# Placing the projection's x tiles first, loading the attention output from ScalarE's queue, and reordering the last four weighing steps

## The chip, the cores and the metric

The kernel runs on one core of a Trainium2 chip. The metric is the device time of one execution in microseconds, as the median of several runs. A core has five engines that run on their own instruction streams: TensorE (PE, matmuls), VectorE (DVE), ScalarE (ACT), GpSimd (POOL) and SyncE (SP). Transfers are issued by SP, ACT or POOL, each on a queue of its own and in the order of its stream, and are carried out by 16 DMA engines that all queues share. An engine that has to wait before it may issue a transfer holds up everything behind it in its stream.

## What is computed

The input `x` has 48 channels of 256 x 256 pixels. Layer 0 normalizes it over groups of channels, makes q, k and v by a pointwise and a depthwise convolution, cuts them into patches of 4 x 4 pixels (4096 tokens), runs 8 heads of attention over the tokens, folds the patches back and projects the result. Layer 1 normalizes again and multiplies along columns, rows and channels in windows of 64. Both layers add their input:

```python
x = x + _L0_conv_ref(_gn(x), w_qkv, w_dw, temperature, w_proj)
    # qkv = dwconv3x3(einsum(x, w_qkv)); q, k l2-normalized per head
    # attn = softmax(einsum('bhcn,bhcm->bhnm', q, k) * temperature)
    # out  = einsum('bhcn,bhnm->bhcm', v, attn); fold; einsum(out, w_proj)
x = x + _L1_conv_ref(_gn(x), Ws, Hs, Cs, 64)
    # einsum('bcphqw,twW,thH,tcC->bCpHqW', windows of x, Ws, Hs, Cs)
```

## The kernel before

The attention takes most of the time. For each of the 8 heads it loops over 16 groups `g` of 256 query tokens; in a group, `scores` (L536) makes the logits (L341) and their exponentials (L545), `normalised` (L554) scales the values (`vn`, L564), and `weigh(h, g, blocks, k)` (L567) multiplies them for `k` = 0 to 3, each `k` covering 1024 of the 4096 tokens (32 matmuls per step, which the trace counts as 64, L574; VectorE adds the result into `oaccs[h, k]`, L585). After the last group of a head, `store(h, m)` (L587) takes 512 tokens at a time, `m` = 0 to 7, where `m` = 2k and 2k + 1 come from step `k`: four transposes (L591), one copy by ScalarE into `oo` (L593; two buffers), and two stores of 96 KB by GpSimd into the DRAM tensor `os_` (L595). In the last group the loop calls `store` one step late (L693): the two pieces of step `k` are stored after step `k + 1`, and pieces 6 and 7 after the loop (L696).

The attention is under a manual schedule: its instructions stand in the order in which they are written. The projection behind it is not: there a scheduler orders each engine's instructions, and derives the waits.

The projection (L702 to L737) runs over 8 tiles `t`. A tile takes 16 rows of each half of the image. Both halves lie side by side on the partitions, 48 channels each, so that a tile has two loads of `pot` (attention output, tile `t` and tile `8 + t` of `os_`; L715) and two of `pxt` (x itself; L716), 768 KB each, all issued by SP. Piece `m` of the attention's store gives tiles 2m and 2m + 1 of `os_`: the first half of tile 0 comes from piece 0, its second half from piece 4. TensorE multiplies (L721), VectorE adds into `pxt` (L728) and takes statistics (L732), and GpSimd stores the two halves of the result into `x1s` (L737), 768 KB each. `pot` and `pxt` have three buffers each in the pool `pj`. Its 96 KB per partition lie, from the bottom up, where the convolution's pool `cv` was (50 KB) and where the attention's pool `ahead` (queries, keys, values) was. The tile that is allocated first lies lowest: `pot` over `cv`, `pxt` over `ahead`.

SP's order as built is: both `pxt` loads of tile 0, the two `pot` loads of tile 0, then tiles 1 and 2 with `pot` and `pxt` in turn; from tile 3 on a `pot` load waits for the matmuls of three tiles before, a `pxt` load for the landing of the x store of three tiles before. Layer 1 (L766 on) begins by reading `x1s` back (L790) once all stores have landed and the statistics are done.

Of the kernel before, what the change touches and what calls it, by code (L numbers as in the profile page):

```python
# [8 lines left out]
F32 = mybir.dt.float32  # L9
# [10 lines left out]
P2 = 2 * C  # L20
# [4 lines left out]
NT = (H // KS) * (W // KS)  # L25
# [13 lines left out]
TP = 256  # L39
# [5 lines left out]
def conv_preact_kernel(  # L45
# [15 lines left out]
    nc = tc.nc  # L61
# [33 lines left out]
    for s in range(2):  # L95
        r = slice(s * C, (s + 1) * C)
        for h in range(NH if s == 0 else H0):
# [3 lines left out]
                in_=w_qkvT.rearrange("c (z h e) -> h c z e", z=3, h=NH)[h],  # L101
# [68 lines left out]
    class Strip:  # L170
# [24 lines left out]
        def store(self):  # L195
            for s, rows in enumerate(both_halves(t1[1], 2 * self.j, 2, base=1)):
                nc.sync.dma_start(out=rows, in_=self.ot[:, 2 * s : 2 * s + 2, :])
# [305 lines left out]
    with tc.tile_pool(name="ahead", bufs=2) as ah, tc.tile_pool(name="ae", bufs=3) as ae, tc.tile_pool(  # L503
# [110 lines left out]
        with tc.manual_schedule():  # L614
            load_query(0, 1)
            block = scores(0, 0)
            for h in range(NH):
                more = h + 1 < NH
                rows = {r: Depthwise(h + 1, r) for r in range(CR + 1)} if more else {}
                for g in range(NG):  # L620
                    p, d, n = rows.get(g - 2), rows.get(g - 1), rows.get(g)

                    if h == 0 and 0 < g <= 6:
                        load_value(0, g + 1)
                    if more and CR + 2 <= g < CR + 6:
                        for m in range(2):
                            load_value(h + 1, (g - CR - 2) * 2 + m)
                    if more and CR + 3 <= g < CR + 6:
                        for m in range(2):
                            load_key(h + 1, (g - CR - 3) * 2 + m)  # L630

                    blocks = [normalised(*block)]
                    block = scores(h, g * G + 1)
                    if more and g == NG - 1:
                        load_key(h + 1, 6)
                        load_key(h + 1, 7, nc.gpsimd)
                    if g + 2 < NG:
                        load_query(h, g + 2)
                    elif more:
                        load_query(h + 1, g + 2 - NG)  # L640
                    if p:
                        p.store((2,))
                    if d:
                        for t in range(1, 4):
                            d.tap(t)
                    second = block
                    if g + 1 < NG:
                        block = scores(h, (g + 1) * G)
                    elif more:
                        block = scores(h + 1, 0)  # L650
                    blocks.append(normalised(*second))
                    if d:
                        for t in range(4, 9):
                            d.tap(t)

                    if g == 0 and rows:
                        rows[0].load()
                    if p:
                        p.high()
                    if d:  # L660
                        d.square()
                    if n:
                        n.first()
                    for k in range(NK):
                        s = (h * NG + g) * NK + k
                        weigh(h, g, blocks, k)
                        if k == 0 and d:
                            d.reduce()
                        if k == 0 and p:
                            p.low(nc.gpsimd)  # L670
                            p.store((0, 1))
                        for w in strips[s]:
                            w.run(big.tile([128, 2, 512], F32, name="big"))
                        for w in strips[s + 2]:
                            w.load()
                        for w in strips[s - 1] if s else []:
                            w.store()
                        if k == 2 and d:
                            d.norm()
                            d.root()  # L680
                        if k == 2 and g + 1 in rows:
                            rows[g + 1].load()
                        if k == 3 and d:
                            d.scale()
                        if h == 0 and 0 < g <= 6 and k == 0:
                            turn(0, g + 1)
                        if more and CR + 2 <= g < CR + 6 and k in (0, 2):
                            turn(h + 1, (g - CR - 2) * 2 + k // 2)

                        if g == 0 and h > 0 and k == 0:  # L690
                            for m in range(6, 8):
                                store(h - 1, m)
                        if g == NG - 1 and k > 0:  # L693
                            for m in range(2 * k - 2, 2 * k):
                                store(h, m)
            for m in range(6, 8):  # L696
                store(NH - 1, m)
    attention.close()
# [5 lines left out]
    with tc.tile_pool(name="pj", bufs=3) as pj, tc.tile_pool(name="pjs", bufs=1) as pjs, tc.tile_pool(  # L704
        name="pps", bufs=3, space=PSUM
    ) as pps, tc.tile_pool(name="pp1", bufs=1, space=PSUM) as pp1:
        st1 = pjs.tile([P2, HALF * W // 512, 6], F32, name="st1")
        ov = os_.rearrange("t (c k) n -> t c k n", k=KK)
        for t in range(HALF // RP):
            ot = pj.tile([P2, KK, NP], F32, name="pot")  # L710
            xt = pj.tile([P2, RP, W], F32, name="pxt")
            for s in range(2):
                r = slice(s * C, (s + 1) * C)
                y0 = s * HALF + t * RP
                nc.sync.dma_start(out=ot[r], in_=ov[s * (NT // 2 // TP) + t])  # L715
                nc.sync.dma_start(out=xt[r], in_=xc[:, y0 : y0 + RP, :])  # L716
            xv = xt.rearrange("p (py ki) (px kj) -> p ki kj py px", ki=KS, kj=KS)
            for ki in range(KS):
                ps = pps.tile([P2, KS, NP], F32, name="pps")
                for i in range(0, KS, 2):  # L720
                    nc.tensor.matmul(  # L721
                        ps[:, i : i + 2, :],
                        lhsT=wp,
                        rhs=ot[:, ki * KS + i : ki * KS + i + 2, :],
                        start=True,
                        stop=True,
                    )
                nc.vector.tensor_add(  # L728
                    xv[:, ki], ps.rearrange("p k (py px) -> p k py px", py=RP // KS), xv[:, ki]
                )  # L730
            for i in range(0, RP, 2):
                nc.vector.bn_stats(  # L732
                    st1[:, (t * RP + i) // 2, :], xt[:, i : i + 2, :].rearrange("p a b -> p (a b)")
                )
            for s in range(2):
                y0 = s * HALF + t * RP
                nc.gpsimd.dma_start(out=x1s[:, y0 : y0 + RP, :], in_=xt[s * C : (s + 1) * C])  # L737

        gm2 = pjs.tile([P2, 64 + C], F32, name="gm2")
        nc.vector.memset(gm2, 0.0)  # L740
        for o in (0, 64):
            nc.vector.tensor_copy(gm2[:, o : o + C], gm[:, 0:C])
        mv1, e1 = group_stats(st1, mean1, rstd1, pjs, pp1)
        pc1 = pp1.tile([64 + C, 1], F32, name="pc1", tag="pstat")
        nc.tensor.matmul(pc1, lhsT=gm2, rhs=e1, start=True, stop=True)
        rstd2 = l1c.tile([64 + C, 1], F32, name="rstd2")
        nc.vector.tensor_scalar_add(rstd2, pc1, EPS)
        nc.scalar.activation(rstd2, rstd2, AF.Sqrt)
        nc.vector.reciprocal(rstd2, rstd2)

        csn = l1c.tile([64 + C, T3 * C], F32, name="csn")
        for s in range(2):
            nc.scalar.dma_start(
                out=csn[s * 64 : s * 64 + C].rearrange("c (t d) -> c t d", t=T3), in_=Cs.rearrange("t c d -> c t d")
            )
            r = slice(s * 64, s * 64 + C)
            nc.vector.tensor_scalar_mul(csn[r], csn[r], rstd2[r])
        mrow = pjs.tile([C, 128], F32, name="mrow")
        nc.vector.tensor_scalar_mul(mrow, ones, mean1[0:C])
        pb1 = pp1.tile([128, T3 * C], F32, name="pb1")  # L760
        nc.tensor.matmul(pb1, lhsT=mrow, rhs=csn[0:C], start=True, stop=True)
        cbias = l1c.tile([128, T3 * C], F32, name="cbias")
        nc.vector.tensor_copy(cbias, pb1)
# [176 lines left out]
```

## Time and profile before

| | us |
|---|---|
| median of 3 runs (3782.36, 3788.41, 3791.38) | 3788.41 |
| profiled execution | 3789.12 |
| its span, first to last instruction | 3787.3 |
| last logits matmul (L341) ends | 3289.27 |
| first matmul of the projection (L721) | 3321.47 |
| last statistics of the projection end (L138 begins) | 3467.71 |
| first load of layer 1 issued (L790) | 3472.86 |

PE is busy 3511.2 us of the span (93%), DVE 2201.6, ACT 1719.0, POOL 599.8. In the projection TensorE's share falls to about half, and its matmuls wait 8 times, 68.3 us in total, for `pot`. A row of the timeline gives the start in us, the duration, the engine (SPq, ACTq: the time in which a queue issued transfers), the line, the operation with output and input tile, how many instructions were merged, and in brackets the idle time before it with what ended it.

### The profile page before, as it was taken

Reading aid. Unit: us, or ns where it says so; the run is one execution under the profiler, and the core shown is the slowest. Engines: PE = TensorE matmul, PEld = TensorE weight load, DVE = VectorE, ACT = ScalarE, POOL = GpSimd, SP = SyncE. Lnnn points to the kernel's source line nnn. Section 1 sums busy time; section 2 is a strip of 40 time slices with the busy share of each in tenths; the row PEclk is TensorE's granted clock in tenths of the full one; section 3 lists DMA queues with packets and bytes.
Section 4 is the critical chain, followed back from the end, with each engine's and each line's share of the span. In section 5 each row is a group of like instructions: output and inputs, shape, how many; then the busy total and the mean of one; then the engine's idle time right before and its main releaser. Section 6 shows DMA issues by size and latency. Waiting matters only on the chain.

```text
span 3787.3 us, 99981 instructions
## 1 busy us (share of the span) xinstructions
PE 3511.2 (93%) x44216; PEld 2913.1 (77%) x44216; DVE 2201.6 (58%) x3520; ACT 1719.0 (45%) x2668; POOL 599.8 (16%) x595
## 2 busy tenths in 40 slices
PE   1867999999999999999999999999999999955998
PEld 0225777788888888888888888888888889812776
DVE  5572775169727962895299439934992222266564
ACT  0224665555545554555455445545554444300222
POOL 0030121012301220121122112211220000000011
PEclk9888999999999999999999999999999999966999
DMA  6575666534533542354244424432443100299784
GB/s 138 168 177 153 185 192 172 167 110 118 116 83 99 125 110 75 104 127 106 81 109 117 100 83 117 116 98 76 123 114 93 41 21 19 44 243 188 122 145 90
DMA packets 307459, 441.64 MB, mean 117 GB/s; under 512 B 98298, under 2 KB 232778, under 8 KB 302792
## 3 DMA queue, kind: packets, MB, share of 16 engines
q1 hardware_dynamic: 253590, 270.32, 27.5%
q0 software_dynamic: 48320, 156.61, 18.5%
q10 hardware_dynamic: 5106, 8.21, 1.0%
q8 instruction: 351, 5.75, 0.6%
q14 instruction: 92, 0.75, 0.1%
HBM read 234.76 MB, written 199.95 MB: 115 GB/s over the span
## 4 chain that ended last, share of the span: by engine, by line
PE 82%; DMA 6%; issue 2%; DVE 1%; SPq 1%; ACT 0%; POOL 0%; ACTq 0%; POOLq 0%
PE big L341 36%; PE big L574 35%; PE pb L838 4%; PE pa L816 2%; PE pc L855 2%; PE big L185 1%; DMA pad<-t 1%; DMA x1s<-pxt 1%; PE pt L591 1%; PE pst L528 1%; DMA pxt<-in_x_dram 1%; DMA pot<-os__70 1%; DMA t<-ot 1%; PE pn L255 1%; DMA qkv<-ol 0%
## 5 line engine op out<-in xcount | busy, mean ns | idle before, releaser
L545 ACT ACTIVATE e<-big,nmx 128x1024 f32<-128x1024 f32 x1024 | 1144.3, 1118 | 842.1 <-PE big L341 631.7
L341 PE MATMUL big<-kt,qt 128*128 128x512 f32 x6144 | 1438.5, 393 | 43.9 <-DMA qt<-qkv 29.9
L574 PEld LDWEIGHTS big<-vn,e 128*64 128x64 f32 x32768 | 1367.6, 137 | 86.1 <-ACT e L545 45.1
L574 PE MATMUL big<-vn,e 128*64 128x96 f32 x32768 | 1425.4, 248 | 7.5 <-ACT ot L188 4.1
L341 PEld LDWEIGHTS big<-kt,qt 128*128 128x128 f32 x6144 | 1145.4, 188 | 306.5 <-issue 44.6
L585 DVE TENSOR_TENSOR oacc<-big,oacc 128x768 f32<-128x768 f32 x480 | 458.2, 955 | 706.2 <-PE big L574 706.2
L236 DVE SCALAR_TENSOR_TENSOR acc<-pad,dwt,acc 126x1024 f32<-126x1024 f32 x600 | 777.2, 1296 | 33.6 <-ACT acc L217 17.2
L294 POOL TENSOR_TENSOR ol<-o,oh 126x1024 fp32r<-126x1024 f32 x80 | 189.4, 2368 | 942.2 <-DVE ss L251 804.7
L558 DVE TENSOR_REDUCE zt<-zs 128x1 f32<-128x4 f32 x256 | 39.0, 152 | 361.3 <-ACT e L545 361.3
L545 ACT ACTIVATION_READ_ACCUMULATOR e<-big,nmx 128x1 f32 x1024 | 196.0, 191 | 0.0
L823 DVE TENSOR_TENSOR lzt<-pa,cbias 128x864 f32<-128x864 f32 (+1 forms) x88 | 137.0, 1627 | 99.7 <-PE pa L816 99.7
L845 ACT COPY lyt<-pb 128x512 f32<-128x512 f32 x144 | 84.5, 586 | 215.7 <-PE pb L838 215.7
L299 POOL DMA_DIRECT2D qkv<-o x70 | 86.1, 1231 | 511.0 <-DVE zu L560 243.6
L595 POOL DMA_DIRECT2D os__70<-oo x128 | 65.1, 515 | 594.0 <-ACT oo L593 593.6
L247 ACT ACTIVATE sq<-acc 126x1024 f32<-126x1024 f32 x75 | 79.3, 1058 | 167.8 <-issue 112.2
L281 DVE TENSOR_TENSOR o<-acc,y 126x1024 f32<-126x1024 f32 x75 | 149.4, 1992 | 0.1
L838 PEld LDWEIGHTS pb<-wsb,lzt 128*64 128x64 f32 x2304 | 126.3, 138 | 29.2 <-issue 21.2
L838 PE MATMUL pb<-wsb,lzt 128*64 128x128 f32 x2304 | 142.7, 280 | 2.5 <-issue 2.4
L721 PE MATMUL pps<-pot,wp 96*96 96x512 f32 x128 | 77.9, 776 | 68.3 <-DMA pot<-os__70 68.3
L188 ACT ACTIVATE ot<-big,bias 108x1024 f32<-108x1024 f32 x64 | 71.1, 1112 | 153.9 <-PE big L185 72.0
L217 ACT ACTIVATE acc<-pad,dwt 126x1024 f32<-126x1024 f32 x75 | 85.3, 1137 | 73.3 <-DMA pad<-t 73.3
L721 PEld LDWEIGHTS pps<-pot,wp 96*96 96x96 f32 x128 | 26.6, 215 | 119.1 <-issue 118.6
(115 smaller groups left out, 1888.4 us busy)
## 6 DMA issues: line engine op xcount, KB each, us to landing
pad<-t SPq DMA_DIRECT2D x80, 761.9 KB
qkv<-ol POOLq DMA_DIRECT2D x80, 504.0 KB, 8.9
qkv<-o POOLq DMA_DIRECT2D x70, 504.0 KB, 6.9
qkv<-oh POOLq DMA_DIRECT2D x70, 504.0 KB, 7.4
t<-ot SPq DMA_DIRECT2D x128, 217.7 KB
qt<-qkv SPq DMA_DIRECT2D x176, 96.0 KB
xs<-in_x_dram SPq DMA_DIRECT2D x128, 96.0 KB
os__70<-oo POOLq DMA_DIRECT2D x128, 96.0 KB, 2.2
```

Of the source, the lines that this page charges most:

```text
L217: nc.scalar.mul(self.acc, self.pad[:, 0:KS, 0:W], dwt[:, self.h, 0:1])
L236: nc.vector.scalar_tensor_tensor(self.acc, self.pad[:, dy : dy + KS, dx : dx + W], dwt[:, self.h, tap : tap + 1], self.acc, ALU.mult, ALU.add,
L281: nc.vector.tensor_tensor(self.o.rearrange("p (a b) x -> p a b x", a=KS), self.acc.rearrange("p a (x b) -> p a b x", b=KS), self.y.rearran ...
L294: eng.tensor_sub(self.ol, self.o, self.oh.bitcast(F32))
L299: eng.dma_start(out=qkv[self.h][i].rearrange("j (c k) n -> (j c) k n", k=KK)[:, :, px], in_=self.o if i == 2 else (self.ol if i else self. ...
L341: nc.tensor.matmul(ps[:, i, :], lhsT=qt[:, r, q0 : q0 + 128], rhs=kts[2 * j + i][:, r // 2, :], start=(r == 0), stop=(r == 2),)
L545: nc.scalar.activation(e[:, j * 1024 : (j + 1) * 1024], ps.rearrange("p a b -> p (a b)"), AF.Exp, bias=nmx[:, b : b + 1], accum_out=zs[:, ...
L574: nc.tensor.matmul(ps[p : p + 64, j // 4, j % 4 * HD : (j % 4 + 1) * HD], lhsT=e[:, mb * 128 + p : mb * 128 + p + 64], rhs=vn, start=(i == 0),
L585: nc.vector.tensor_add(oaccs[h, k], ps[:, :, : 4 * HD], oaccs[h, k])
L721: nc.tensor.matmul(ps[:, i : i + 2, :], lhsT=wp, rhs=ot[:, ki * KS + i : ki * KS + i + 2, :], start=True, stop=True,)
L823: nc.vector.tensor_tensor(zv[:, :, y0 : y0 + n, :], pa[:, :, : n * T3 * C].rearrange("p s (y k) -> p s y k", y=n), cbias.rearrange("p (u v ...
L838: nc.tensor.matmul(pb[s * WS : (s + 1) * WS, i, :], lhsT=zts[u][:, t * C + c + i, :], rhs=wsb[:, t, :], start=True, stop=True,)
```

## The change

Three edits. In the projection, `pxt` is allocated ahead of `pot`, so that it lies over `cv` and `pot` over `ahead`; SP issues the `pxt` loads, ScalarE the `pot` loads. In the last group of the last head the steps run in the order 0, 2, 1, 3, and the pieces of the step before are stored after each: pieces 0 and 1, then 4 and 5, then 2 and 3, then 6 and 7.

```diff
-                    for k in range(NK):
+
+                    steps = (0, 2, 1, 3) if not more and g == NG - 1 else range(NK)
+                    for i, k in enumerate(steps):
                         s = (h * NG + g) * NK + k
                         weigh(h, g, blocks, k)
...
-                        if g == NG - 1 and k > 0:
-                            for m in range(2 * k - 2, 2 * k):
-                                store(h, m)
+                        if g == NG - 1 and i > 0:
+                            for m in range(2):
+                                store(h, 2 * steps[i - 1] + m)
             for m in range(6, 8):
                 store(NH - 1, m)
...
         for t in range(HALF // RP):
+            xt = pj.tile([P2, RP, W], F32, name="pxt")
             ot = pj.tile([P2, KK, NP], F32, name="pot")
-            xt = pj.tile([P2, RP, W], F32, name="pxt")
             for s in range(2):
                 r = slice(s * C, (s + 1) * C)
                 y0 = s * HALF + t * RP
-                nc.sync.dma_start(out=ot[r], in_=ov[s * (NT // 2 // TP) + t])
                 nc.sync.dma_start(out=xt[r], in_=xc[:, y0 : y0 + RP, :])
+                nc.scalar.dma_start(out=ot[r], in_=ov[s * (NT // 2 // TP) + t])
```

## The prediction

> **What bounds the kernel now.** I read the page first, then the busy time of the engines in short windows round the end of the attention, then the timelines of the queues there. The page says that TensorE carries the kernel and gives way in one place:
>
> ```profile
> span 3787.3 us, 99981 instructions
> PE   1867999999999999999999999999999999955998
> DMA  6575666534533542354244424432443100299784
> ```
>
> One slice is 94.7 us. Up to slice 35 TensorE sets the pace and nothing in the change adds work to it. Slices 36 and 37 (3314 to 3503 us) are the projection: PE falls to 5 tenths and DMA goes to 9. Ahead of them DMA stands at 0 in two slices. The windows show where the one turns into the other (us, then busy time of PE, PEld, DVE, ACT, POOL with counts, granted clock, DMA share, GB/s):
>
> ```profile
> 3287.00:3291.00 4.00, 2.59 (x15) 1.74 (x13) 0.38 (x3) 3.21 (x6) 0.00 (x0) 1.00 0.00 0
> 3291.00:3295.00 4.00, 3.54 (x46) 3.54 (x48) 0.80 (x5) 0.00 (x0) 0.00 (x0) 0.57 0.77 135
> ...
> 3299.00:3303.00 4.00, 3.08 (x64) 2.71 (x61) 0.46 (x1) 1.07 (x2) 2.04 (x4) 1.00 0.73 175
> ...
> 3307.00:3311.00 4.00, 1.90 (x30) 1.53 (x26) 0.96 (x1) 0.00 (x0) 0.67 (x2) 1.00 0.61 129
> 3311.00:3315.00 4.00, 1.94 (x8) 1.45 (x8) 0.00 (x0) 1.07 (x2) 2.03 (x4) 0.63 0.23 67
> ...
> 3345.00:3355.00 10.00, 0.28 (x1) 0.31 (x2) 6.57 (x9) 0.00 (x0) 1.03 (x2) 0.56 0.98 320
> 3355.00:3365.00 10.00, 9.34 (x16) 2.95 (x15) 5.00 (x3) 0.00 (x0) 0.00 (x0) 0.76 1.07 247
> 3365.00:3375.00 10.00, 0.26 (x1) 0.29 (x2) 7.35 (x10) 0.00 (x0) 1.03 (x2) 0.58 0.95 197
> ```
>
> From 3315 on the DMA share is about 1.0 whatever the compute engines do: the projection is bound by transfers. A tile takes 20 us there (the x stores of tiles 2 and 3 are issued at 3367.90 and 3387.91), while VectorE needs 7.7 + 4.8 us and PE 9 to 10 us of it. But between 3291 and 3315 the DMA engines have holes, because SP waits. SP's queue there, and ScalarE's:
>
> ```profile
> 3291.60 0.79 SPq L716 DMA_DIRECT2D pxt<-in_x_dram  x2
> 3303.35 12.08 SPq L715 DMA_DIRECT2D pot<-os__70  x3
> 3315.47 0.44 SPq L716 DMA_DIRECT2D pxt<-in_x_dram  x1
> ```
>
> ```profile
> 3299.06 1.07 ACT L593 COPY oo<-pt 96x512 f32<-96x512 f32 x2 [8.54 <-PE pt L591]
> 3304.74 1.07 ACT L593 COPY oo<-pt 96x512 f32<-96x512 f32 x2 [4.62 <-PE pt L591]
> 3311.81 1.07 ACT L593 COPY oo<-pt 96x512 f32<-96x512 f32 x2 [6.00 <-DMA os__70<-oo]
> 3315.40 0.58 ACT L593 COPY oo<-pt 96x512 f32<-96x512 f32 x1 [2.52 <-DMA os__70<-oo]
> 3319.64 0.58 ACT L593 COPY oo<-pt 96x512 f32<-96x512 f32 x1 [3.66 <-DMA os__70<-oo]
> ```
>
> SP stands behind the attention output of the upper half, which is stored by the third round of copies, and the x loads of tiles 1 and 2 stand behind SP. The copies themselves run in rounds, since `oo` has two buffers: each waits until a store of the round before has landed.
>
> **What the change does not move.** The built programs of both kernels have the same waits at the first x load: the last logits matmul (L341) and the last `vn` (L564, ended 3291.4 us), because they are taken for the whole pool, and the pool still covers the attention's tiles. SP's own waits show how long it stood there (waiter, what it waited for, us in total, times, longest):
>
> ```profile
> SPq L716 <- DVE vn L564: 41.2, 1, 41.2
> ```
>
> Had the placement lifted that wait, six loads of 0.786 MB could go out from 3250 on beside a DMA share of 0.01 (3250 to 3291), and 4.72 MB at 200 GB/s, 24 us, would be hidden. As built it is worth 0, and the first x load stays at 3291.6.
>
> **Part 1: six x loads go out at 3291.6, not two.** SP now holds x loads alone. Tiles 0 to 2 are free, so four loads that were issued from 3315.47 on come some 24 us earlier. The hole they fill, from both sides: by share, (0.23 + 0.04 + 0.27 + 0.03 + 0.39 + 0.77) x 4 = 6.9 us of DMA time unused between 3291 and 3315; by bytes, (135 + 164 + 175 + 186 + 129 + 67) x 4 = 3.42 MB moved, which at the 200 GB/s of the load-only windows (197, 202) is 17 us, so 7 us unused. That is the most that this part can give at the engines' rate.
>
> **Part 2: the copies get slower.** The attention output (2 x 0.098 MB per copy) now shares the DMA engines with 4.72 MB of x loads, which at 164 GB/s (3295 to 3299, almost only x) last to 3320 us. The rows' landing times for these stores are 1.9 at least, 5.1 in the median, 16.9 at most; the last belongs to the round of 3320.5, behind a full queue. So I put the first round's stores at 3302.4 + 16.9 = 3319.3. Output loads on ScalarE's queue also stand between the copies: the order there is copies 0 and 1, load of tile 0 lower half, copies 4 and 5, load of tile 1 lower half, copies 2 and 3, load of tile 0 upper half, copies 6 and 7, then all others. Each such issue costs about 0.4 us on SP and waits only for a landing that the next copy waits for too. Rounds two and three then cost the 6.0 us wait and 1.07 us of copies each: last copy at 3319.5 + 2 x 7.1 = 3333.7, instead of 3319.64. Price from both sides: 0 if stores land as before, 14 us as taken. The first projection matmul waits for this last copy in both programs, so it goes from 3321.47 to about 3335.
>
> **Part 3: steps 0, 2, 1, 3.** No work is added or removed: the same 256 matmuls (10.7 us) and 32 transposes on PE. Piece 4, from which tile 0's upper half is loaded, goes out in round two instead of three, one round or 7 us earlier (3304.74 to 3311.81). But on ScalarE's queue that load stands behind the copies of round three, so it still goes out after them, and the first matmul waits for round four anyway. Worth 0 here; without it tile 0's load would come a round later, 7 us, still before the matmul may start.
>
> **The sum.** What counts in a stretch bound by transfers is how much has been moved at one time. At 3335 before: the six windows just summed and the next five (271, 160, 158, 168, 274) give 1887 x 4 = 7.55 MB, less 1.57 MB of attention output, 5.98 MB = 7.6 loads of 0.786 MB. After: six x loads and three output loads, 9 in all, with the output stores 8.65 MB in 44 us, or 197 GB/s, which is the rate seen. So the lead is 1.4 loads. A tile has four loads in 20 us, 5 us each with its share of stores: 7 us. Counted by bytes at 3347, when the first x store is now issued, the lead is smaller: 10.56 MB before, 8.65 + 12 x 0.2 = 11.05 MB after, 0.49 MB or 2 us at 234 GB/s (28.8 MB in the 123 us up to 3470). I take 5, nearer to the upper end, since the stores ride beside loads at 288 to 320 GB/s. At the tail, output loads no longer come last; VectorE starts tile 7 at 3455.28, 3.7 us after the first matmul of that tile: 0 to 3.7, I take 2. Together 7 us. After 3470 nothing changes. The profiled execution took 3789.12 (span 3787.3): 3782.1. The median lies 0.7 below: 3788.41 - 7 = 3781.4.
>
> The Trainium skill, page "DMA: Bandwidth & Descriptors", section "Rules for kernel authors", says that spreading transfers over the issuing engines brings no bandwidth, only the issue time. The trace's x loads at the start, on two queues, moved 193 to 211 GB/s in windows of 10 us from 20 to 70 us, against 197 to 202 on one queue here; by the rule the sum stays at 7, by these rows it could be 4 us more, which is the first rival.
>
> **The rivals.** *Two queues load faster.* The five windows of the early x loads (193, 211, 210, 206, 204) mean 205 GB/s, the load-only windows here 198; 25.2 MB of loads take 127 us at the one and 123 at the other. For it: same shape, both halves in flight. Against it: no stores ran then. Further 4 us, and the tail's full 3.7 and lead's 7: 3774.
>
> *The lead is given back.* The first x store comes 13 us later (3347, not 3334), so the stores bunch, and the next x loads wait for them (SP's longest wait in total is 86.0 us, for x stores). For it: the total of bytes is the same, and by bytes the lead is 2 us. Against it: DMA was at 1.0 without any help. 3787.
>
> *The copies become the bound, slower.* Place: ScalarE's queue between 3300 and 3350. If rounds two and three also take the 16.9 us, the last copy comes at 3319.5 + 2 x 18 = 3355. Nine loads are done at 3333, the next three stand behind that copy, so the DMA engines idle for some 20 us, less the lead of 7: 13 us slower, 3801. It decides once the last copy is later than about 3341, where nine loads were done before (1.1 MB after 3335 at 0.2 MB/us). For it: 16.9 was seen. Against it: by then the x queue is empty and only one output load is in flight, as in the row with 6.00.
>
> **How the numbers follow.** Forecast 0.50 at 3781.4, own range 3777.4 to 3785.4; faster loads 0.19 at 3774; given back 0.14 at 3787; copies 0.17 at 3801. A measurement of this kernel can tell about 0.2%, 7.6 us, from no change; the forecast of 7 lies just inside it, so 0.22 of its 0.50 counts as faster, 0.28 as same. Faster 0.22 + 0.19 = 0.41, same 0.28 + 0.14 = 0.42, slower 0.17. The range leaves out most of the last case and the fast end of the second: 3771 to 3793.
>
> **What would show it.** Six x loads issued within 4 us of 3291.6; if they come from 3250 on, my reading of the wait is wrong, and the gain is nearer to 24. DMA share near 1.0 in every window from 3291 to 3335. Last copy (L593) near 3334; later than 3341 means slower. First matmul of the projection just behind it. Nine loads landed by 3335. Tiles still 20 us apart from tile 3 on; 18 or less means that two queues load faster. VectorE's last tile starting within 1 us of its x load, near 3448. The stage after it should look as before, shifted.

## The result, and the profile after

22 runs of each kernel: 3776.8 us after (3765.17 to 3785.14), 3779.45 us before (3768.63 to 3791.38). The ratio is 0.9991, 95% interval [0.9982, 1.0]: a gain of 0.1%, at most 0.2%, perhaps nothing. The time predicted was 3781.4, with 3777.4 to 3785.4 as the forecast's own range and 3771 to 3793 as the whole; the measured one lies 0.6 us below the former and inside the latter. The gain predicted was 7 us, the measured one is 2.65. The three runs of before that were known ahead lay above the median of the 22, and the profiled execution (3789.12) lay 9.7 us above it. The profiled execution of after took 3777.19.

The page of the kernel after, span, TensorE and DMA over the 40 slices (one slice is 94.4 us):

```profile
span 3775.4 us, 99983 instructions
...
PE   1867999999999999999999999999999999955998
...
DMA  6575676534533542354244424542543100199784
```

At this scale nothing moved: the same two slices with PE at 5, the same 9 of DMA. The windows of 10 us from the start of the last `vn` show what did. First the kernel after (us, then busy time of PE, PEld, DVE, ACT, POOL with counts, granted clock, DMA share, GB/s):

```profile
3289.22:3299.22 10.00, 8.96 (x191) 8.48 (x191) 2.61 (x6) 1.06 (x2) 2.03 (x4) 1.00 0.89 159
3299.22:3309.22 10.00, 6.43 (x71) 5.78 (x73) 0.96 (x1) 0.00 (x0) 0.00 (x0) 0.66 1.03 202
3309.22:3319.22 10.00, 1.55 (x16) 0.92 (x12) 0.96 (x1) 0.58 (x1) 1.02 (x2) 0.63 1.02 198
3319.22:3329.22 10.00, 2.04 (x8) 1.29 (x8) 0.00 (x0) 1.16 (x2) 2.02 (x4) 0.50 0.77 137
3329.22:3339.22 10.00, 1.90 (x5) 1.04 (x6) 0.00 (x0) 1.66 (x3) 2.64 (x6) 0.50 0.65 179
3339.22:3349.22 10.00, 10.00 (x21) 3.67 (x20) 6.89 (x5) 0.00 (x0) 0.40 (x1) 0.83 0.98 189
```

The same windows of the kernel before, from its own last `vn`:

```profile
3291.13:3301.13 10.00, 9.67 (x174) 9.37 (x176) 2.62 (x6) 1.07 (x2) 1.20 (x3) 0.83 0.87 161
3301.13:3311.13 10.00, 6.22 (x108) 5.36 (x104) 1.92 (x2) 1.07 (x2) 2.87 (x6) 1.00 0.75 156
3311.13:3321.13 10.00, 1.94 (x8) 1.45 (x8) 0.00 (x0) 3.12 (x5) 3.66 (x8) 0.55 0.74 172
3321.13:3331.13 10.00, 9.18 (x16) 3.16 (x16) 5.73 (x4) 0.39 (x1) 0.40 (x1) 0.77 0.96 158
3331.13:3341.13 10.00, 5.86 (x9) 2.18 (x10) 8.79 (x11) 0.00 (x0) 1.03 (x2) 0.66 1.05 229
```

The hole in the second and third window is filled (0.75 and 0.74 became 1.03 and 1.02), and another of the same size stands in the fourth and fifth (0.96 and 1.05 became 0.77 and 0.65). Over these 50 us the shares that lack to 1 add up to 0.68, 6.8 us, before, and to 0.69, 6.9 us, after; the bytes to 8.76 MB before ((161 + 156 + 172 + 158 + 229) x 10 us) and 8.75 MB after. The lead that the prediction counted on is gone by the time the projection starts.

Where it went is in ScalarE's timeline of the kernel after (start, duration, engine, line, operation, in brackets the idle time ahead and what ended it):

```profile
3295.49 1.06 ACT L593 COPY oo<-pt 96x512 f32<-96x512 f32 x2 [6.89 <-PE pt L591]
3308.11 0.33 ACTq L718 DMA_DIRECT2D pot<-os__70  x1
3311.61 0.58 ACT L593 COPY oo<-pt 96x512 f32<-96x512 f32 x1 [15.05 <-DMA os__70<-oo]
3323.15 0.58 ACT L593 COPY oo<-pt 96x512 f32<-96x512 f32 x1 [10.97 <-DMA os__70<-oo]
...
3331.33 0.58 ACT L593 COPY oo<-pt 96x512 f32<-96x512 f32 x1 [6.64 <-DMA os__70<-oo]
...
3337.73 0.58 ACT L593 COPY oo<-pt 96x512 f32<-96x512 f32 x1 [5.32 <-DMA os__70<-oo]
3337.75 1.26 ACTq L718 DMA_DIRECT2D pot<-os__70  x3
```

Most copies wait for a small store of an earlier round to land, and the first round's stores now land behind x loads: the copies of the second round wait 15.05 and 10.97 us for them. Before, the second round waited for no landing (only 4.62 us for its transposes), and the later ones 6.00, 2.52 and 3.66. The last copy starts 48.5 us behind the last `vn`, not 28.5, and the first matmul 49.2 us behind it, not 30.3. That alone would be a loss of 19 us. The rest of the stage gives it back. The page's group of the projection's matmuls, first before, then after (busy time, mean ns | idle time ahead, what ended most of it):

```profile
L721 PE MATMUL pps<-pot,wp 96*96 96x512 f32 x128 | 77.9, 776 | 68.3 <-DMA pot<-os__70 68.3
```

```profile
L723 PE MATMUL pps<-pot,wp 96*96 96x512 f32 x128 | 75.9, 759 | 41.5 <-DVE pxt L730 36.1
```

Before, every tile's matmuls waited for the attention output, 68.3 us in total. After, they wait 36.1 us for VectorE, which reads the buffers that they write, and once, 5.4 us, for the last copy; no matmul has the output load as the wait that ended last. What these waits are worth is read from VectorE, which ends each tile: its adds and statistics take 12.4 us a tile, 99 us in all, in both kernels, and its idle time comes on top. Its waits for x loads, before and after (us in total, times, longest):

```profile
DVE pxt L728 <- DMA pxt<-in_x_dram: 31.5, 5, 8.3
```

```profile
DVE pxt L730 <- DMA pxt<-in_x_dram: 16.1, 3, 7.6
```

With 8.4 us that the profile puts down to "issue" and 2.8 for a matmul, VectorE stands 42.7 us behind its first add before, and 16.1 after. These 26.6 us are nearly all of the difference between the two profiles from the first matmul on (146.3 and 119.5); in the repeats below, e5 and e6, the idle times are 36.6 and 20.9. So the wait that ends last before is mostly that for x, not that for the attention output. The order of issue fits one queue as the source of both: before, SP issues an x, an output, an x and an output load within 3 us (3353.51 to 3356.16), once an x store has landed; after, ScalarE's output loads (3360.69, 3372.55) go out between SP's x loads (3365.19, 3387.04). VectorE's timeline of the kernel after, at the tail:

```profile
3433.14 7.73 DVE L730 TENSOR_TENSOR pxt<-pps,pxt 96x1024 f32<-96x1024 f32 x4
3440.77 4.83 DVE L734 BATCH_NORM_STATS2 st<-pxt 96x6 f32<-96x512 f32 x8
3445.52 7.58 DVE L730 TENSOR_TENSOR pxt<-pps,pxt 96x1024 f32<-96x1024 f32 x4
3452.98 4.85 DVE L734 BATCH_NORM_STATS2 st<-pxt 96x6 f32<-96x512 f32 x8
3457.87 1.88 DVE L138 BATCH_NORM_AGGREGATE mv<-st 96x2 f32<-96x384 f32 x1
```

No idle time in brackets: the last two tiles run at VectorE's own pace, 12.4 us each, where tiles of the kernel before came some 20 us apart in its first profile and 17 to 18 in the repeats.

So the stage falls into two parts, and the change moves them against each other. For every run, from its one profiled execution, in us: the start of the last copy (in e7, e8 and e12, where the last two merge in one row, of the last pair) and of the first projection matmul, behind the start of the last `vn`; from that matmul to the end of the statistics; and the whole, `vn` to statistics.

| run | output loads on | last copy | first matmul | matmul to statistics | whole | ratio to before, 95% |
|---|---|---|---|---|---|---|
| before | SP | 28.5 | 30.3 | 146.3 | 176.6 | |
| e1_place_only | SP | 28.9 | 30.8 | 138.8 | 169.6 | 1.0008 [0.9995, 1.0022] |
| e5_repeat_before | SP | 28.2 | 30.3 | 140.1 | 170.4 | one run |
| after | ScalarE | 48.5 | 49.2 | 119.5 | 168.7 | 0.9991 [0.9982, 1.0] |
| e6_repeat_after | ScalarE | 48.1 | 48.8 | 124.5 | 173.3 | one run |
| e2_queue_only | ScalarE | 48.6 | 54.9 | 122.4 | 177.3 | 1.0017 [1.0006, 1.0028] |
| e3_order_only | SP | 44.8 | 45.5 | 130.4 | 175.9 | 1.0018 [1.0005, 1.003] |
| e11_x_first_sp | SP | 56.9 | 57.6 | 139.5 | 197.1 | 1.0063 [1.0046, 1.008] |
| e4_own_pool | ScalarE | 31.5 | 32.2 | 124.5 | 156.7 | 0.9985 [0.9975, 0.9996] |
| e9_own_pool_again | ScalarE | 31.3 | 32.0 | 122.6 | 154.6 | 0.9975 [0.996, 0.999] |
| e10_own_pool_pots_sp | SP | 41.7 | 42.4 | 139.4 | 181.8 | 1.004 [1.0025, 1.0055] |
| e7_spare_sp | SP | 20.8 | 40.4 | 134.7 | 175.1 | 1.0037 [1.0025, 1.005] |
| e8_own_spare_sp | SP | 15.2 | 24.0 | 140.6 | 164.6 | 0.9991 [0.9977, 1.0004] |
| e12_own_spare | ScalarE | 22.1 | 28.3 | 121.7 | 150.0 | 0.9945 [0.993, 0.9959] |

With the output loads on ScalarE's queue the second part takes 119.5 to 124.5 us in six profiles, on SP's queue 130.4 to 146.3 in eight, and on ScalarE's it is no longer when the first matmul comes at 28.3 us than when it comes at 54.9. The first part depends on what stands ahead of the small stores. The time behind the statistics is 316.5 to 321.1 us everywhere.

### The profile page after: what moved, and what is told of

Read it like the earlier page. It is cut to its first block, busy times and chain, and to the rows that moved or that the text cites. A ratio compares the mean times of both kernels' runs of the same rounds, so it can differ in the third digit from the quotient of the medians.

```text
span 3775.4 us, 99983 instructions
## 1 busy us (share of the span) xinstructions
PE 3510.2 (93%) x44216; PEld 2911.9 (77%) x44216; DVE 2200.4 (58%) x3520; ACT 1718.1 (46%) x2668; POOL 598.8 (16%) x595
## 4 chain that ended last, share of the span: by engine, by line
PE 84%; DMA 5%; issue 1%; DVE 1%; ACT 0%; SPq 0%; POOL 0%; ACTq 0%; POOLq 0%; DVEq 0%
PE big L341 37%; PE big L574 36%; PE pb L840 4%; PE pa L818 2%; PE pc L857 2%; PE big L185 2%; DMA os__70<-oo 1%; DMA xs<-in_x_dram 1%; PE pt L591 1%; PE pst L528 1%; PE pn L255 1%; DMA pxt<-in_x_dram 1%; DMA x1s<-pxt 1%; DMA kt<-qkv 0%; DVE pxt L730 0%
## 5 line engine op out<-in xcount | busy, mean ns | idle before, releaser
L840 PEld LDWEIGHTS pb<-wsb,lzt 128*64 128x64 f32 x2304 | 125.5, 138 | 28.9 <-issue 20.5
L723 PE MATMUL pps<-pot,wp 96*96 96x512 f32 x128 | 75.9, 759 | 41.5 <-DVE pxt L730 36.1
L315 POOL DMA_DIRECT2D kt<-qkv x44 | 22.8, 529 | 569.3 <-PE big L341 552.9
```

Source lines behind the costliest of these rows:

```text
L840: nc.tensor.matmul(pb[s * WS : (s + 1) * WS, i, :], lhsT=zts[u][:, t * C + c + i, :], rhs=wsb[:, t, :], start=True, stop=True,)
```

## The experiments

**Each of the three edits alone.** e1: the two allocation lines swapped.

```diff
+            xt = pj.tile([P2, RP, W], F32, name="pxt")
             ot = pj.tile([P2, KK, NP], F32, name="pot")
-            xt = pj.tile([P2, RP, W], F32, name="pxt")
```

> The kernel before with one edit: the x tiles are allocated ahead of the attention output's tiles, all loads stay on SP in the old order. My theory: the waits belong to the whole pool, so the first x load still goes out right behind the last vn, within 1 us of it, and nothing changes: 0 us, the stretch from the last vn to the last statistics of the projection about 176 us as before (3291.4 to 3467.7), last copy some 29 us behind the vn. Rival (the placement frees the x loads): x loads go out up to 41 us ahead of the last vn, and the stretch is some 20 us shorter.

Measured: 3778.24 against 3778.32 us. No effect of the placement shows (0.05% less to 0.22% more). Its edit changes addresses alone, SP issues its loads in the same order as before, and the first x load goes out 0.5 us behind the start of the last `vn` in both; so its profile is taken here as a second look at the kernel before: `vn` to statistics 169.6 us, where the first had 176.6.

e2: the queue, with the loads in the order of the change, without the other two edits.

```diff
-                nc.sync.dma_start(out=ot[r], in_=ov[s * (NT // 2 // TP) + t])
                 nc.sync.dma_start(out=xt[r], in_=xc[:, y0 : y0 + RP, :])
+                nc.scalar.dma_start(out=ot[r], in_=ov[s * (NT // 2 // TP) + t])
```

> The kernel before with one edit: the attention output is loaded from ScalarE's queue. My theory: this is the part that works. Six x loads go out within 4 us of the last vn, copies are delayed as in the changed kernel (last copy 45 to 50 us behind the vn, not 29), the stretch from the last vn to the last statistics is 168 us as in the changed kernel (176 before), and the time 3 to 8 us below before. Without the order of steps 0, 2, 1, 3 tile 0's upper half is stored in round three and loaded behind the last copy, so the first matmul comes up to 8 us later than in the changed kernel (49 us behind the vn there). Rival (the order of steps is what pays): about 176 us.

Measured: 3783.95 against 3778.32, slower, where the theory had 3 to 8 us gained. TensorE's timeline of e2, the first projection matmul:

```profile
3345.67 14.84 PE L721 MATMUL pps<-pot,wp 96*96 96x512 f32 x27 [12.54 <-DMA pot<-os__70]
```

Tile 0's second half comes from piece 4, which in the old order goes out so late that its load is issued behind the last copy; the matmul waits for that load, 54.9 us behind `vn`. In the kernel after it waits for the last copy only, 49.2. The order is worth 5.7 us at this place, and 0.26% in the ratios (1.0017 to 0.9991, each to its own runs of before).

e3: the order alone, with the diff of the change.

> The kernel before with one edit: steps 0, 2, 1, 3 and the stores in that order; loads all on SP, old allocation. My theory: SP's wait for tile 0's upper half ends one round of copies earlier (at about 3304.7 + 7 instead of 3315 on the scale of before), so the four x loads go out some 7 us earlier, and part of the hole of 7 us is filled without any contention for the copies: the stretch from the last vn to the last statistics 171 to 174 us, time 2 to 5 us below before. Rival (worth nothing by itself, as I had priced it): 176 us.

Measured: 3785.03 against 3778.32, slower, where the theory had 2 to 5 us gained. ScalarE's timeline of e3, the third and fourth round of copies:

```profile
3310.89 1.07 ACT L593 COPY oo<-pt 96x512 f32<-96x512 f32 x2 [6.42 <-DMA os__70<-oo]
3329.20 0.58 ACT L593 COPY oo<-pt 96x512 f32<-96x512 f32 x1 [17.25 <-DMA os__70<-oo]
```

With piece 4 stored a round earlier, SP issues the loads that stood behind it 22.0 us behind `vn`, just as the third round's copies start (21.4); before, they went out at 24.3, behind copies that start at 20.7. So the third round's stores now stand behind loads (seven of 0.786 MB are issued between 3311.4 and 3316.7), and the fourth round waits 17.25 us for them, where it waited 2.52 and 3.66. The same edit is a gain with one queue arrangement and a loss with the other.

**x in a pool of its own.** e4 is the kernel after with `pxt` in a pool opened first, so that it covers only the convolution's tiles, which are free long before; e9 is e4 once more, on another chip beside runs of before there (e10, e11 and e12 too).

```diff
-    with tc.tile_pool(name="pj", bufs=3) as pj, ...
+    with tc.tile_pool(name="px", bufs=3) as px, tc.tile_pool(name="pj", bufs=3) as pj, ...
-            xt = pj.tile([P2, RP, W], F32, name="pxt")
+            xt = px.tile([P2, RP, W], F32, name="pxt")
```

> The changed kernel with one more edit: the x tiles get a pool of their own, which is opened first and lies over the convolution's pool alone. My theory (waits are taken for a whole pool): now the first six x loads need nothing of the attention's last groups; they go out more than 40 us ahead of the last vn, under the attention, at no cost there. Copies then meet an almost empty set of DMA engines: last copy 25 to 30 us behind the vn, first matmul 27 to 32, and 4.72 MB (24 us at 200 GB/s) are moved ahead of time: the stretch from the last vn to the last statistics 145 to 155 us, time 15 to 25 us below before. Rival (the projection is bound by what follows the copies, the early loads are only waiting there): 165 us or more, time as in the changed kernel.

> The same program as the earlier run with its own pool for the x tiles (ratio 0.9985), so that the version that beats both kernels rests on two measurements. Theory (the hidden x loads are worth 6 to 8 us in time): 0.9977 to 0.9992 of the time before. Rival (that run was the fast end of the spread between runs, as the first profile before was the slow end): 0.9995 or more. In the profile: first x loads near 2910, last copy 31 to 33 us and first projection matmul 32 to 34 us behind the last vn in both.

Measured: 3770.03 against 3778.32, and 3770.27 against 3778.03: 8.3 and 7.8 us gained, where the theory of e4 had 15 to 25 and that of e9 6 to 8. SP's queue in e9:

```profile
2867.85 0.45 SPq L719 DMA_DIRECT2D pxt<-in_x_dram  x1
```

The first x load goes out some 430 us ahead of the last `vn` (3296.34), and nothing stands ahead of the small stores: the last copy comes at 31.3 us, the first matmul at 32.0. Placing the tiles over a free region does not free them: in the kernel after the first x load still waits for the last `vn` (41.2 us in SP's waits, as before). What frees them is a pool that covers that region alone. The first matmul comes 17 us earlier than in the kernel after, and the stage is 15 us shorter by the means of two profiles each (171.0 to 155.7); the ratios lie lower by 0.0006 and 0.0016, 2 to 6 us. Part of the rest may lie in which executions were profiled: those of the kernel after were 4.6 us slower on average than its median of 22, those of e4 and e9 1.5 us faster than theirs. What is left is not accounted for.

**Repeats, unchanged.** Because one profile of before had started the sum, each kernel was profiled again.

> The kernel before once more, for a second profile. My theory (the 176.6 us from the last vn to the last statistics in the first profile were a slow execution; the tiles' distance of 20 us is not fixed): some 168 to 172 us, with the copies and the first matmul at the same distance from the vn as before (28.5 and 30.3 us) and the later tiles 17 to 18 us apart, as in the kernel with the placement alone. Rival (the placement, by its addresses, made the transfers faster): 176 us again.

> The changed kernel once more. My theory: last copy 45 to 50 us behind the last vn and first matmul right behind it, as in the first profile (48.5 and 49.2); the stretch to the last statistics 166 to 172 us, so that it differs from the kernel before by 0 to 4 us, which is the measured gain of 2.7 us. Rival (the stage really gains 8 us, and the gain is lost elsewhere): 8 us below the repeat of the kernel before, with a longer stretch in front or behind.

Three profiles of the program before have 176.6, 169.6 and 170.4 us from `vn` to statistics, mean 172.2; two of after 168.7 and 173.3, mean 171.0. The 7.9 us between the first two profiles lie within the spread of executions; the means differ by 1.2, in keeping with the measured 2.65.

**Are the copies the bound?** e7 and e8 write the last eight copies into a spare tile of exponentials instead of the two `oo` buffers, so that no copy waits for a landing; both load the attention output from SP, the x loads of tiles 0 to 2 ahead of it. e7 has the change's one pool, e8 the pool of its own for x.

```diff
+            if (h, "last") in values:
+                oo = values[h, "last"][:HD, m * 512 : (m + 1) * 512]
+            else:
-            oo = asm.tile([HD, 512], F32, name="oo", bufs=2)
+                oo = asm.tile([HD, 512], F32, name="oo", bufs=2)
...
+                    if not more and g == NG - 1:
+                        values[h, "last"] = ae.tile([128, NT], F32, name="e")
```

> The changed kernel with the copies freed: the last head's eight pieces are copied into a buffer of the exponentials that is free by then, not into two oo buffers, so that no copy waits for a store to land; and the attention output is loaded from SP behind the x loads of tiles 0 to 2, so that no load stands between the copies. My theory (the chain of copies gave the lead back): last copy 20 to 24 us behind the vn, not 48; first matmul limited by tile 0's loads, 32 to 38; stretch to the last statistics 6 to 12 us below the changed kernel's repeat, time 6 to 12 us below before. Rival (the transfers bound the stage in any case): first matmul earlier, but the stretch within 3 us of the changed kernel's.

> The same two edits on the kernel with a pool of its own for x (x loads far ahead), output loads on SP. My theory: copies done 20 to 22 us behind the last vn, first matmul 24 to 28 us behind it (32.2 with the chain of copies), stretch to the last statistics 148 to 156 us (156.7), time 10 to 16 us below before. Rival (transfers alone bound it, and the chain of copies cost nothing there): 156 us and the time of the kernel with the pool of its own, 0.15 percent below before.

Measured: 1.0037 and 0.9991, where the theory had 6 to 12 and 10 to 16 us gained. Last copies that start at 20.8 and 15.2 us do not make the kernel faster while the output loads are on SP: the second part stays at 134.7 and 140.6 us. These two left open whether the queue or the rearranged loads did it, hence the next pair.

**The queue by itself.** e10 is e9, and e11 the kernel after, with the output loads on SP again; in e11 the six x loads are issued ahead of them, as in the kernel after.

```diff
-                nc.scalar.dma_start(out=ot[r], in_=ov[s * (NT // 2 // TP) + t])
+                nc.sync.dma_start(out=ot[r], in_=ov[s * (NT // 2 // TP) + t])
```

> The version with its own x pool, with the attention output loaded from SP's queue again, behind its tile's x; nothing else differs. Theory A (on one queue a load that waits for a buffer or for a landing holds up the loads behind it, whatever the lead at the start): the distance from the first to the last x store goes from 107 us to 112 to 129 us, and the ratio from 0.9985 to 0.9993 to 1.0005. Theory B (the queue of the output loads matters only while the copies run, and here the x loads are out by then): 107 us and 0.9985 again.

> The kernel after, but with the output loads on SP: the x loads of tiles 0 to 2 are issued first, then tile by tile output load and next x load on the one queue; the order 0, 2, 1, 3 and the two oo buffers stay. Theory A (the second queue is what the change lives on, not the early x loads): 1.0010 to 1.0035. Theory B (six x loads at the last vn are what it lives on): 0.9985 to 0.9995. In both the copies are slow as in the kernel after, 44 to 50 us to the last one, with the first matmul just behind it.

Measured: 3792.93 us against 3770.27 for e9, and 1.0063 against 0.9991 for the kernel after. Theory A of both, by more than it had priced in time; the distance from first to last x store in e10, 122.8 us, lies in its range of 112 to 129. The matmuls' group on the page of e9, of e10 and of e11:

```profile
L725 PE MATMUL pps<-pot,wp 96*96 96x512 f32 x128 | 75.1, 754 | 44.9 <-DVE pxt L732 39.6
```

```profile
L725 PE MATMUL pps<-pot,wp 96*96 96x512 f32 x128 | 76.6, 766 | 66.4 <-DMA pot<-os__70 48.8
```

```profile
L733 PE MATMUL pps<-pot,wp 96*96 96x512 f32 x128 | 76.7, 766 | 75.6 <-DMA pot<-os__70 49.1
```

The wait for the attention output comes and goes with the queue. SP's waits in e10 say why (waiter, what it waited for, us in total, times, longest):

```profile
SPq L719 <- DMA x1s<-pxt: 76.4, 6, 21.2
SPq L720 <- DMA os__70<-oo: 63.4, 3, 50.9
...
SPq L720 <- PE pps L725: 28.8, 2, 26.6
```

On one queue an x load that waits for a store of three tiles before (76.4 us) holds up the output load behind it, and an output load that waits for the matmuls to free its buffer (26.6 us) holds up the x loads. Windows of e10, then of e11, where the DMA engines run dry:

```profile
3337.93:3347.93 10.00, 7.61 (x13) 2.84 (x14) 3.72 (x2) 1.86 (x2) 1.01 (x2) 0.68 0.14 46
```

```profile
3356.57:3366.57 10.00, 10.00 (x22) 3.58 (x20) 8.48 (x5) 0.00 (x0) 0.00 (x0) 0.90 0.28 52
```

Both end ahead of the first x store (3352.94 and 3366.88): all three tiles are loaded, the next output load waits for tile 0's matmuls, and the x loads behind it for the landing of tile 0's store. e9 and the kernel after have no such window ahead of their tails (the lowest shares, from 10 us behind the last `vn` on, are 0.72 and 0.65), since ScalarE issues the output loads of tiles 1 and 2 behind its copies, when the small stores are out. That also keeps these loads from the small stores: the last copy comes at 31.3 us in e9 and 41.7 in e10, at 48.5 in the kernel after and 56.9 in e11. The dry windows are not all of it: e8, also on SP's queue, has none from 10 us behind the last `vn` to its tail (0.72 at the lowest) and still takes 140.6 us. What e8, e10 and e11 share is VectorE's idle time behind its first add, 34 to 35 us, spent waiting for matmuls, which wait for output loads; in e9 and e12 it is 19.1 and 18.0, for x loads. e8 and e12 differ in the queue alone, though they ran on two chips.

**Both parts mended.** e12 is e9 with the spare tile for the copies.

> The version with its own x pool and the output loads on ScalarE's queue, with the last eight copies written into a spare tile instead of two oo buffers, so that no copy waits for a landing. Theory A (from the first matmul on the transfers bind; earlier copies only move the hole): last copy 15 to 20 us behind the last vn instead of 31.5, and the ratio stays at 0.9980 to 0.9990. Theory B (the rounds of copies still cost what they delay the first matmul by): first matmul 8 us earlier, ratio 0.9960 to 0.9975.

Measured: 3758.64 us against 3778.03, ratio 0.9945 [0.993, 0.9959], and 11.6 below e9 on the same chip: better than both theories had it. ScalarE's timeline of e12:

```profile
3303.05 1.07 ACT L596 COPY e<-pt 96x512 f32<-96x512 f32 x2 [6.94 <-PE pt L591]
...
3306.79 1.07 ACT L596 COPY e<-pt 96x512 f32<-96x512 f32 x2 [2.68 <-PE pt L591]
...
3310.59 1.07 ACT L596 COPY e<-pt 96x512 f32<-96x512 f32 x2 [2.73 <-PE pt L591]
3318.46 0.31 ACTq L725 DMA_DIRECT2D pot<-os__70  x1
3318.81 1.07 ACT L596 COPY e<-pt 96x512 f32<-96x512 f32 x2 [7.16 <-DMA os__70<-e]
```

The copies wait for the transposes, not for landings; only the last two stand behind an output load that waits for one. The first matmul comes 3.7 us earlier than in e9, not 8. Windows of e12 and, below, of e9, from 10 to 40 us behind the last `vn`:

```profile
3306.72:3316.72 10.00, 5.40 (x85) 4.50 (x82) 1.42 (x2) 2.13 (x4) 3.75 (x8) 0.96 1.07 170
3316.72:3326.72 10.00, 1.73 (x2) 0.68 (x3) 0.00 (x0) 1.07 (x2) 2.35 (x5) 0.50 0.93 255
3326.72:3336.72 10.00, 10.00 (x22) 3.70 (x20) 7.79 (x5) 0.00 (x0) 0.00 (x0) 0.86 1.06 209
```

```profile
3306.34:3316.34 10.00, 5.78 (x81) 4.71 (x79) 1.43 (x2) 1.67 (x3) 3.04 (x6) 0.79 0.82 155
3316.34:3326.34 10.00, 1.09 (x4) 0.64 (x4) 0.00 (x0) 1.08 (x2) 2.02 (x4) 0.50 0.72 176
3326.34:3336.34 10.00, 8.01 (x14) 3.00 (x15) 4.08 (x3) 0.58 (x1) 1.01 (x2) 0.69 0.85 170
```

The hole that the change had only moved is closed. The profiles explain 4.6 of the 11.6 us (154.6 to 150.0); e12's profiled execution was the slowest of its six, 3766.72 us, so the rest may be that; this stays open.

## Why the prediction was right, and where it was wrong

*What does not move.* Right: the first x load stayed at the last `vn`, and no effect of the placement shows (e1). The remark that freeing the loads would hide 24 us of transfers was right as to the transfers; the stage gains about 15 us by it and the time 2 to 6 (e4 and e9 against the kernel after).

*Part 1.* Five x loads went out in 2.4 us from 3289.69 and the sixth at 3302.41, having waited 10.3 us for an earlier one to land; not all six within 4 us, as stated. The hole of the second and third window was filled.

*Part 2.* Right in its mechanism, too small in size: the last copy 48.5 us behind `vn`, where the working has 42.6 (3333.7 less 3291.1). The later rounds cost 8.2 and 6.4 us each, near the 7.1 taken; the term that was too small is the landing of the first round's stores: the last of them landed 24.7 us after its issue (3298.33 to 3323.05), where 16.9 had been taken as the most. The working also has the first matmul waiting for the last copy in both programs; before, its wait of 7.09 us ended with an output load.

*Part 3, "Worth 0 here".* Wrong. The step says that without the new order tile 0's load would come "still before the matmul may start". That load goes out behind the last copy, and the first matmul comes 6.3 us behind the start of that copy, having waited for the load (e2). The order is worth 0.26% beside ScalarE's queue, and costs 0.18% beside SP's (e3).

*The sum.* Its lead is the term that was mis-sized. "A tile has four loads in 20 us" counted 1.4 loads ahead at 3335 and took 5 us. By bytes there is no lead at 50 us (8.75 against 8.76 MB), because the copies that Part 2 delays open a second hole. And the 20 us of a tile were taken as the pace of the DMA engines, since their share was 1.0; they were not. With the output loads on a queue of their own, tiles of the kernel after follow one another in (164.2 - 86.0) / 5 = 15.6 us on average from tile 2 to tile 7, by the issue of their x stores, and the last ones in 12.4 (16.5 on average in the repeat; 17.7 and 17.8 in e5 and e1, on one queue). The sum of 7 us with 2 for the tail is in truth a loss of 18.5 in the first part (means 30.5 to 49.0) and a gain of 19.7 in the second (141.7 to 122.0). The gain forecast was 4.4 us too large and the base 9.0 too high, so the time came out 4.6 too high. It came out within the range because both parts were missed by about as much: that is luck, and not what the sum describes. By the gain alone, 2.65 lies nearer to the 1.4 of "the lead is given back" than to 7.

*The base.* All durations came from one execution, 9.7 us slower than the median of the 22 runs, and this stage took it 6 to 7 us longer than the other two profiles of before (176.6 against 169.6 and 170.4).

*The signs.* The last copy came before 3341, with the first matmul just behind it, as stated. The DMA share did not stay near 1.0 (0.77 and 0.65), and VectorE's last tile followed the one before it without a wait, not its x load. Tiles 18 us apart or less were to mean that two queues load faster; they were, but so they were in e5 and e1, on one queue, so that this sign told nothing.

*The rivals.* "Two queues load faster" saw the second part, at 4 us instead of some 20, and by another cause: where only x loads run the rate is the same 202 and 198 GB/s. The Trainium skill, page "DMA: Bandwidth & Descriptors", section "Rules for kernel authors", says that spreading transfers over the issuing engines doesn't help bandwidth and only saves issue time; those windows agree as to bandwidth. The pairs after and e11, e4 or e9 and e10, e12 and e8 differ by 15 to 20 of the 140 us from the first matmul to the statistics, which the waits above put down to what stands behind a waiting load. "The copies become the bound" saw the first part; its threshold, a last copy at 3341, was not reached (3337.7). "The lead is given back" is what the first 50 us show; SP's wait for x stores, 86.0 us before, grew to 122.5. Whether, beyond the order of the loads, a second queue also changes how loads and stores share the engines was not separated: at a share near 1 the windows of e9 carry 208 to 321 GB/s from 60 to 130 us, those of e10 162 to 315 from 80 to 130.

## What to carry to other kernels

A DMA share of 1.0 does not say that bytes set the pace: look at what the consumer waits for, tile by tile, and at what each waiting load holds up on its queue. Loads moved forward land ahead of whatever small stores are on the way; if those stores release the next step, the hole that was filled opens again behind them, so let the loads go before the stores exist, or free the step from the landing. And a tile that is placed over free memory starts no earlier while its pool covers memory that is in use.

## What the hardware showed beyond what was expected

Small stores (96 KB) behind queued loads of 768 KB each were waited for 15 to 17 us (15.05 after, 17.25 in e3), though they are issued from another queue, GpSimd's; with the loads out beforehand the same waits are 4 to 7 us (e9: 4.83, 4.32, 6.79, 5.28). The last of these stores in the kernel after landed 24.7 us after its issue. The same program's stage, `vn` to statistics, varies by 7 us from execution to execution (169.6 to 176.6), more than twice the effect measured.
